# A four-layer conditional residual block: second sums computed already turned, identity inside the adapter weights, and another order of the first part

## The chip, the cores and the metric

The kernel runs on one core of one Trainium2 chip. The metric is the device time of one execution in microseconds; the number quoted for a kernel is the median of its runs. A profile is one further execution, recorded by the hardware profiler, and it comes with its own time.

## The reference, cut to what matters

The input x has 32 sequences of 32 tokens with 512 features, all in float32. Four layers each add their result to x:

```python
x = x + einsum('bct,bcd->bdt', x, w_mix[cond])                          # 1: mixes the 32 tokens of a sequence
x = x + einsum('bsi,oi->bso', x, W) + 0.5 * ((x @ lora_A[lab]) @ lora_B.T)   # 2: base product and LoRA
x = x + einsum('bsi,boi->bso', x, weight[adapter_id])                   # 3: one 512x512 adapter per sequence
x = x + attention(x)     # 4: q, k, v projections, norms, rotary turn, paged cache of 512 keys, output product
```

Layers 1 to 3 and a part of layer 4's value projection are the first part of the kernel, which the change rewrites. The adapter weights are 32 times 1 MB, one for each sequence, chosen by an index.

## The kernel before, in words

The 1024 tokens are cut into eight tiles of 128 tokens (four sequences a tile). `xs` holds all tiles with tokens on the partitions. Three stages follow one another: the first part (layers 1 to 3 and seven tiles of one value chunk), a second part of query, key and value projections in blocks of two tiles (line L393), and the attention with the output product.

For tile t the first part does the following.

- `mixers(t)` (L674, L681) builds on VectorE a 128x128 block matrix of the four gathered mixing weights with the identity added; `mix(t)` (L688) multiplies with it, so that the residual is in the product, and leaves the tile turned (features on the partitions) in `x1t`.
- `low_1(t)` (L707) multiplies by the LoRA matrices of all five labelers; VectorE picks one (L711, L718) into a wide tile whose other columns are zero.
- `base(t)` (L726) multiplies 128 tokens by `wb`, which has the identity on its diagonal, with 512 output columns moving; L729 turns the low values, L731 scales them, L732 adds the LoRA product. VectorE copies the sum back to `xs` (L734).
- `flip_2(t)` (L697, x2t) turns the sum with four TensorE transposes, and ScalarE copies it.
- `adapt(t)` (L751) multiplies each sequence's 32 tokens by its own adapter weight, four column groups side by side; VectorE adds the product to `xs` (L758).
- `transposed(t, x3t)` (L697) turns the result for the projections; after every second tile `token_sums` (L375 to L378) forms four sums on GpSimd.
- `project` (L312) computes a value tile of chunk NCH - 2, copied by ScalarE (L322) and stored by GpSimd's queue (L327).

TensorE and VectorE run the first part in the order in which the code is written (`manual_schedule`); ScalarE, GpSimd and the SP queue are ordered by the planner of the framework. In the second part and in the attention, all engines run in written order. The written loop of the first part takes, at step n, mix(n), base(n-1), flip_2(n-2), low_1(n), the turn of tile n-4, adapt(n-3) and value tiles from n = 6 on. `angles()` computes the rotary sines and cosines: VectorE first (L764 to L781), then ScalarE (L778 to L783), then eight products on GpSimd (L789 to L792).

All large loads go through the SP queue. An adapter weight `wa` has eight buffers, so `load_adapt` for tile t+2 waits until adapt(t) has read its buffers. `load_qkv` loads the value chunk's weight (1024 KB), and `load_pair(0)` the first pair of the second part (2 MB in four loads).

Of the kernel before, what the change touches and what calls it, by code (L numbers as in the profile page):

```python
# [12 lines left out]
F32 = mybir.dt.float32  # L13
# [7 lines left out]
P = 128  # L21
# [38 lines left out]
def cond_resid_kernel(  # L60
# [227 lines left out]
    taken = []  # L288

    def accumulator(name: str, long: bool = False):  # L290
        taken.append(name)
        pool = ps_m if long or len(taken) % 3 else ps_n
        return pool.tile([P, HID], F32, tag="mm", name=name)


    x3_all = xp.tile([P, KC, NT * P], F32, name="x3t")

    def x3t(t: int):
# [331 lines left out]
    with ExitStack() as p1:  # L630
# [8 lines left out]
        lb = w1p.tile([P, HID], F32, name="lb")  # L639
        nc.gpsimd.memset(lb, 0.0)  # L640

        ones = w1p.tile([P, HID], F32, name="ones")
        nc.vector.memset(ones, 1.0)
# [7 lines left out]
        mgs, x1ts, lows, x2ts, was = {}, {}, {}, {}, {}  # L651


        wide = [w1p.tile([P, P], F32, name=f"low_{i}") for i in range(3)]
        for low in wide:
            nc.gpsimd.memset(low, 0.0)

        def gather_mix(t: int):
            mg = sp.tile([P, S], F32, tag="mg", name=f"mg_{t}", bufs=4)
# [10 lines left out]
        def mixers(t: int):  # L670


            md = sp.tile([P, BT, S], F32, tag="md", name=f"md_{t}", bufs=3)
            nc.vector.tensor_tensor(  # L674
                md,
                mgs.pop(t).unsqueeze(1).to_broadcast([P, BT, S]),
                quarter.unsqueeze(2).to_broadcast([P, BT, S]),
                ALU.mult,
            )
            mds[t] = md.rearrange("p j s -> p (j s)")  # L680
            nc.vector.tensor_tensor(mds[t], mds[t], ident, ALU.add)  # L681

        def mix(t: int):

            md = mds.pop(t)
            px = ps_tr.tile([P, KC, P], F32, tag="tr", name=f"x1t_ps_{t}")
            for k in range(KC):
                nc.tensor.matmul(  # L688
                    px[:, k, :], xs[:, t, k * P : (k + 1) * P], md, start=True, stop=True
                )  # L690
            x1ts[t] = sp.tile([P, KC, P], F32, tag="x1t", name=f"x1t_{t}", bufs=3)
            nc.scalar.copy(x1ts[t], px)
# [9 lines left out]
        which = w1p.tile([P, NT, NL], F32, name="which")  # L702

        def low_1(t: int):
            plo = ps_m.tile([P, HID], F32, tag="mm", name=f"low_ps_{t}")[:, : NL * R]
            for k in range(KC):
                nc.tensor.matmul(  # L707
                    plo, x1ts[t][:, k, :], la[:, k, :], start=(k == 0), stop=(k == KC - 1)
                )
# [12 lines left out]
        def base(t: int):  # L722
            xt = x1ts.pop(t)
            pb = accumulator(f"base_{t}")
            for k in range(KC):
                nc.tensor.matmul(pb, xt[:, k, :], wb[:, k, :], start=(k == 0), stop=False)  # L726
                if k == KC - 2:
                    plt = ps_tr.tile([P, P], F32, tag="tr", name=f"lowt_ps_{t}")
                    nc.tensor.transpose(plt, lows.pop(t), ident)  # L729
                    lowt = sp.tile([P, P], F32, tag="lowt", name=f"lowt_{t}")  # L730
                    nc.scalar.mul(lowt, plt, LORA_SCALING)  # L731
            nc.tensor.matmul(pb, lowt, lb, start=False, stop=True)  # L732

            nc.vector.tensor_copy(xs[:, t, :], pb)  # L734

        def flip_2(t: int):
            x2ts[t] = sp.tile([P, KC, P], F32, tag="x2t", name=f"x2t_{t}")
            transposed(t, x2ts[t], "x2t")

        def load_adapt(b: int):  # L740
            was[b] = wap.tile([P, KC, HID], F32, tag="wa", name=f"wa_{b}")
            dma_picked(was[b], w_adapt, pk[0:1, b : b + 1], "a p k o -> p (a k) o")

        def adapt(t: int):
            xt = x2ts.pop(t)
            pa2 = accumulator(f"adapt_{t}")

            for k in range(KC):
                for j in range(BT):
                    r = slice(j * S, (j + 1) * S)  # L750
                    nc.tensor.matmul(  # L751
                        pa2[r, :],
                        xt[:, k, r],
                        was[t * BT + j][:, k, :],
                        start=(k == 0),
                        stop=(k == KC - 1),
                    )
            nc.vector.tensor_tensor(xs[:, t, :], xs[:, t, :], pa2, ALU.add)  # L758

        def angles():  # L760

# [12 lines left out]
            for part in (PI_A, PI_B, PI_C):  # L774
# [7 lines left out]
            cs = w1p.tile([P, NT, H2], F32, name="cs")  # L782
            nc.scalar.activation(  # L783
                cs.rearrange("p t f -> p (t f)"), turns, AF.Sin, bias=half_pi, scale=-1.0
            )
# [15 lines left out]
        loads = ExitStack()  # L801
        loads.enter_context(tc.issue_after(gate.ins))
        load_x(2)
        nc.sync.dma_start(out=lb[:R, :], in_=lora_b)
        load_x(3)
        for b in range(BT):
            load_adapt(b)
# [15 lines left out]
        with tc.manual_schedule(engines={mybir.EngineType.PE, mybir.EngineType.DVE}):  # L823

            idle = ps_tr.tile([P, HID], F32, tag="tr", name="idle_ps")
            for n in (HID, HID, P, P, P, P, P, P):
                nc.tensor.matmul(idle[:, :n], ones[:, :P], ones[:, :n], start=True, stop=True)

            def ahead_of(t: int):
                if t + 3 < NT:  # L830
                    gather_mix(t + 3)
                if t < NT:
                    mixers(t)

            def adapt_and_load(t: int):
                adapt(t)
                if t + 2 < NT:
                    for j in range(BT):
                        load_adapt((t + 2) * BT + j)
# [12 lines left out]
            low_1(1)  # L852
            base(0)
            mix(2)
            low_1(2)
            ahead_of(3)
            flip_2(0)
            base(1)
            for n in range(3, NT + 4):
                if n < NT:  # L860
                    mix(n)
                if n - 1 < NT:
                    base(n - 1)
                if n - 2 < NT:
                    flip_2(n - 2)
                if n < NT:
                    low_1(n)
                    ahead_of(n + 1)
                if NT <= n:
                    project(NCH - 2, n - 6 + (n == NT + 3))  # L870
                if n == NT + 2:
                    project(NCH - 2, NT - 3)
                if 0 <= n - 4 < NT:
                    transposed(n - 4, x3t(n - 4), "x3t")
                    if n % 2:
                        token_sums((n - 4) // 2)
                if n - 3 < NT:
                    adapt_and_load(n - 3)
                if n == 3:
                    constants()  # L880
                    angles()
                if 6 <= n < NT:
                    project(NCH - 2, n - 6)
                if n == 4:
                    with tc.issue_after(picked[-1]):
                        load_qkv(NCH - 2)
                if n == 6:
                    with tc.issue_after(picked[-1]):
                        load_pair(0)

    nc.gpsimd.dma_start(out=x_d.rearrange("t p d -> p t d"), in_=xs)
    first_part.close()
# [507 lines left out]
```

## Time and profile before

| what | value |
|---|---|
| median of 3 runs | 1136.5 us (1135.73 to 1137.75) |
| the profiled execution's own time | 1136.3 us |
| its span | 1134.5 us |
| granted TensorE clock, mean | 1.0 |
| first part ends (first L393 product begins) | 121.66 us |
| adapters begin, tiles 0 to 7 | 31.14, 42.17, 53.61, 64.64, 79.10, 95.01, 103.04, 114.11 us |
| DMA bytes over the span | 259.24 MB, mean 229 GB/s |

The page gives each engine's busy time over the span; TensorE's matmuls are pipelined and their ends are modelled. Every float32 matmul appears as two passes, so "x32" beside an adapter means 16 matmuls. In a timeline the columns are start and length in us, engine, line, operation, what is written from what, the shape, the count, and in brackets the idle time ahead with what ended it. In a table of windows each engine's busy time and instruction count stand in the order PE, PEld (weight load), DVE (VectorE), ACT (ScalarE), POOL (GpSimd), then the granted clock, the mean busy share of the 16 DMA engines and GB/s.

### The profile page before, as it was taken

What the parts mean: (1) busy time and instruction counts of PE and PEld (TensorE: products, weight loads), DVE (VectorE), ACT (ScalarE), POOL (GpSimd) and SP (SyncE); (2) the same over time, 40 slices, a digit from 0 to 9 for tenths busy, and PEclk for the clock granted to TensorE, in tenths of its full rate; (3) what the DMA queues carried; (4) which work ended last, traced back from release to release, by engine and by line L of the source; (5) the groups of instructions that cost most, each with busy time, mean ns of one, the idle gap of its engine ahead of it and who ended that gap; (6) DMA issues with size and microseconds to landing.
All of it is one profiled execution on the core that took longest, in us unless ns stands there. A gap on an engine that the chain in (4) does not pass through costs nothing.

```text
span 1134.5 us, 19093 instructions
## 1 busy us (share of the span) xinstructions
PE 1119.1 (99%) x5480; PEld 738.0 (65%) x5480; DVE 812.3 (72%) x1674; ACT 739.3 (65%) x1885; POOL 561.0 (49%) x730
## 2 busy tenths in 40 slices
PE   8999999999999899999999999999999999999998
PEld 5554444444444688777777777777777777777766
DVE  2510688887877578878778878887877787877861
ACT  1211377676666677678877777777777877777850
POOL 3411689899798455543444344334433443344410
PEclk9999999999999999999999999999999999999999
DMA  8998447688886687778767756775777676766600
GB/s 319 391 419 352 177 130 211 162 246 221 210 234 176 203 267 264 254 255 301 241 210 243 260 190 212 264 244 183 234 239 240 199 234 223 253 201 212 231 28 10
DMA packets 173355, 259.24 MB, mean 229 GB/s; under 512 B 31522, under 2 KB 130466, under 8 KB 168770
## 3 DMA queue, kind: packets, MB, share of 16 engines
q1 hardware_dynamic: 152226, 184.22, 51.4%
q0 software_dynamic: 20016, 71.97, 17.8%
q10 hardware_dynamic: 1008, 1.84, 0.4%
q8 instruction: 44, 0.72, 0.3%
q14 instruction: 61, 0.50, 0.1%
HBM read 228.46 MB, written 37.88 MB: 235 GB/s over the span
## 4 chain that ended last, share of the span: by engine, by line
PE 61%; DVE 2%; ACT 0%; issue 0%; DVEq 0%
PE o_ps L1103 19%; PE f_ps L1180 18%; PE s_ps L1023 11%; PE s_ps L1024 9%; PE o_ps L1123 2%; PE pn_ps L1090 1%; PE f_ps L1200 1%; PE f_ps_last L1200 1%; DVE placed L1079 1%; PE qkv L312 1%; DVE pr L1032 0%; DVE turned L1061 0%; ACT placed L1075 0%; DVE os L1139 0%; DVE ot L1160 0%
## 5 line engine op out<-in xcount | busy, mean ns | idle before, releaser
L1075 ACT COPY placed<-turned 32x512 f32<-32x512 f32 x524 | 322.6, 616 | 30.2 <-DVE turned L1061 24.2
L1103 PEld LDWEIGHTS o_ps<-vt,placed 128*128 128x128 f32 x2048 | 264.2, 191 | 110.9 <-issue 74.6
L1032 DVE CUSTOM_DVE_ANT_0 pr<-s_ps,mask,rq 128x544 f32<-128x544 f32 x256 | 200.4, 783 | 129.6 <-PE s_ps L1024 106.4
L1048 ACT ACTIVATE pr<-pr,low 128x544 f32<-128x544 f32 x256 | 191.6, 748 | 142.6 <-DVE low L1032 116.1
L1077 POOL COPY placed<-turned 32x512 f32<-32x512 f32 x279 | 169.6, 608 | 222.2 <-DVE turned L1061 173.5
L1103 PE MATMUL o_ps<-vt,placed 128*128 128x128 f32 x2048 | 272.0, 276 | 3.9 <-DVE os L1139 3.3
L1180 PE MATMUL f_ps<-wo,ot 128*128 128x512 f32 x480 | 240.6, 593 | 0.0
L1061 DVE STREAM_TRANSPOSE turned<-pr 128x512 f32<-128x512 f32 x256 | 178.6, 698 | 0.1
L1023 PE MATMUL s_ps<-kt,qt 128*128 128x288 f32 x512 | 174.0, 421 | 4.2 <-DVE low L1032 2.4
L1024 PE MATMUL s_ps<-kt,qt 128*128 128x256 f32 x512 | 152.3, 379 | 0.0
L252 POOL DMA_INDIRECT vt<-in_v_cache_dram,v_idx x128 | 124.3, 971 | 36.6 <-issue 25.7
L1024 PEld LDWEIGHTS s_ps<-kt,qt 128*128 128x128 f32 x512 | 97.3, 190 | 26.8
L438 POOL TENSOR_TENSOR ra<-ra,rs 128x512 f32<-128x512 f32 x80 | 103.8, 1303 | 10.7 <-DVE rs L433 8.1
L1079 DVE COPY placed<-turned 32x512 f32<-32x512 f32 x221 | 101.9, 461 | 5.6
L1180 PEld LDWEIGHTS f_ps<-wo,ot 128*128 128x128 f32 x480 | 86.9, 190 | 25.1 <-issue 13.9
L1086 POOL COPY pq<-pr 128x128 f32<-128x128 f32 x64 | 18.5, 288 | 151.6 <-ACT pr L1048 111.2
L1023 PEld LDWEIGHTS s_ps<-kt,qt 128*128 128x128 f32 x512 | 78.2, 191 | 17.3 <-DVE low L1032 6.1
L451 ACT ACTIVATE sq<-x 128x128 f32<-128x128 f32 x256 | 76.2, 301 | 19.8 <-DVE x L409 13.6
L548 ACT COPY r<-m 128x512 f32<-128x512 f32 x80 | 46.3, 579 | 52.4 <-PE m L393 50.4
L393 PE MATMUL m<-t_pair,x_sums 128*128 128x512 f32 x160 | 75.4, 594 | 0.7 <-ACT r L548 0.7
L393 PE MATMUL m<-w_pair,x3t 128*128 128x512 f32 x160 | 75.2, 592 | 0.0
L393 PE MATMUL m<-w_pair,x_sums 128*128 128x512 f32 x160 | 72.1, 593 | 0.0
(129 smaller groups left out, 1231.8 us busy)
## 6 DMA issues: line engine op xcount, KB each, us to landing
kt<-in_k_cache_dram SPq DMA_DIRECT2D x512, 128.0 KB
wa<-in_w_adapt_dram SPq DMA_DIRECT2D x32, 1024.0 KB
q_d<-st SPq DMA_DIRECT2D x128, 128.0 KB
qt<-q_d SPq DMA_DIRECT2D x64, 256.0 KB
w_pair<-in_w_qkv_dram SPq DMA_DIRECT2D x20, 512.0 KB
o_d<-in_w_o_dram SPq DMA_DIRECT2D x16, 512.0 KB
wo<-o_d SPq DMA_DIRECT2D x16, 512.0 KB
k_d<-st SPq DMA_DIRECT2D x32, 128.0 KB
```

What stands on the lines that cost most here:

```text
L252: nc.gpsimd.indirect_dma_start(out=vts[b][:, c, :], out_offset=None, in_=v_cache, in_offset=bass.IndirectOffsetOnAxis(ap=v_idx[:, at : at ...
L393: nc.tensor.matmul(ps, of[:, k], by[:, k], start=(not more and k == 0), stop=(k == KH - 1), skip_group_check=more,)
L1023: nc.tensor.matmul(ps[:, first:L], q, kt4[:, :N_LOW, g, :], start=True, stop=True)
L1024: nc.tensor.matmul(ps[:, L : first + LT], q, kt4[:, N_LOW:, g, :], start=True, stop=True)
L1032: nc.vector.tensor_tensor_reduce(pr, ps[:, first : first + LT], mask, rqs[b][:, g // QUAD, u : u + 1], 3.0e38, ALU.add, ALU.min, low,)
L1048: nc.scalar.activation(pr, pr, AF.Exp, bias=low, scale=-1.0, accum_out=dens[quad][:, u : u + 1])
L1061: nc.vector.transpose(part, pr)
L1075: nc.scalar.copy(dst, src)
L1077: nc.gpsimd.tensor_copy(dst, src)
L1079: nc.vector.tensor_copy(dst, src)
L1103: nc.tensor.matmul(po, pt[:, c, :], vt[:, c, g * D : (g + 1) * D], start=(c == 0 and q == 0), stop=(c == L // P - 1 and q == 1),)
L1180: nc.tensor.matmul(pfs[t][:, :HID], ots[t, h // HALF][:, h % HALF, :], wo(h), start=(h == 0), stop=(h == (HQ if t < NT - 1 else HALF) - 1),)
```

## The change

- `base` works on two tiles and computes the sum already turned: pieces of `wb` are the stationary side and 256 tokens move. The low values are repeated four times across the columns, so that after one transpose each of four groups of 32 partitions holds them, and the LoRA product is four matmuls of 32 rows each. ScalarE copies the four sums into `x2t`. `flip_2` and the copy to `xs` are gone.
- `with_identity` adds the identity to the four adapter weights of a tile on VectorE, two operations a weight; `adapt` then yields x plus the product, and VectorE copies it to `xs`.
- The written order of the first part is a list: two base products come ahead of the first adapter, mixes and low products run in twos, `angles` moves behind adapt(4), and value tiles 3 to 6 stand behind the last adapter.
- `load_qkv` follows the loads of tile 2, and `load_pair(0)` the loads of tile 7. `lora_b` is loaded in four pieces. Buffers of `mg` and `md` grow by one; accumulators of base are in one pool, those of low products, adapters and value tiles in another.

```diff
-    def project(c: int, t: int, slots=()):
-        ps = accumulator(f"qkv_{c}_{t}", True)
+    def project(c: int, t: int, slots=(), pool=ps_m):
+        ps = pool.tile([P, HID], F32, tag="mm", name=f"qkv_{c}_{t}")
...
-            lows[t] = wide[t % 3]
+            lows[t] = sp.tile([P, KC, R], F32, tag="low", name=f"low_{t}")
             nc.vector.tensor_reduce(
-                lows[t][:, :R], picked.rearrange("p l r -> p r l"), AX.X, ALU.add
+                lows[t][:, 0, :], picked.rearrange("p l r -> p r l"), AX.X, ALU.add
+            )
+            nc.vector.tensor_copy(
+                lows[t][:, 1:, :], lows[t][:, 0, :].unsqueeze(1).to_broadcast([P, KC - 1, R])
             )
...
+        def base(g: int):
+            xt = x1ts.pop(g)
+            pbs = [
+                ps_m.tile([P, HID], F32, tag="mm", name=f"base_{g}_{j}")[:, : 2 * P]
+                for j in range(KC)
+            ]
+            lowt = sp.tile([P, 2 * P], F32, tag="lowt", name=f"lowt_{g}")
+            for j in range(KC):
+                for k in range(KC):
+                    nc.tensor.matmul(pbs[j], wb[:, k, j * P : (j + 1) * P], xt[:, k, :],
+                                     start=(k == 0), stop=False)
+                if j == KC - 2:
+                    plt = ps_tr.tile([P, 2 * P], F32, tag="tr", name=f"lowt_ps_{g}")
+                    for u in range(2):
+                        low = lows.pop(2 * g + u).rearrange("p j r -> p (j r)")
+                        nc.tensor.transpose(plt[:, u * P : (u + 1) * P], low, ident)
+                    nc.scalar.mul(lowt, plt, LORA_SCALING)
+            x2ts[g] = sp.tile([P, KC, 2 * P], F32, tag="x2t", name=f"x2t_{g}")
+            for j in range(KC):
+                r = slice(j * R, (j + 1) * R)
+                nc.tensor.matmul(pbs[j], lb[r, :], lowt[r, :], start=False, stop=True)
+            for j in range(KC):
+                nc.scalar.copy(x2ts[g][:, j, :], pbs[j])
...
+        def with_identity(t: int):
+            for b in range(t * BT, (t + 1) * BT):
+                w = was[b].rearrange("p k o -> p (k o)")
+                step = HID + P
+                most = w[:, : (KC - 1) * step].rearrange("p (k o) -> p k o", o=step)[:, :, :P]
+                last = w[:, (KC - 1) * step :]
+                one = ident.unsqueeze(1).to_broadcast([P, KC - 1, P])
+                nc.vector.tensor_tensor(most, most, one, ALU.add)
+                nc.vector.tensor_tensor(last, last, ident, ALU.add)
...
-            nc.vector.tensor_tensor(xs[:, t, :], xs[:, t, :], pa2, ALU.add)
+            nc.vector.tensor_copy(xs[:, t, :], pa2)
...
+            ahead_of(3)
+            ahead_of(4, 5)
             base(0)
+            mixed(2, 3)
+            ahead_of(6)
+            with_identity(0)
             base(1)
+            adapt(0)
+            loads(2)
+            with tc.issue_after(picked[-1]):
+                load_qkv(NCH - 2)
+            with_identity(1)
+            turned(0)
+            adapt(1)
+            loads(3)
+            mixed(4, 5)
+            turned(1)
+            with_identity(2)
+            constants()
+            adapt(2)
+            loads(4)
+            ahead_of(7)
+            with_identity(3)
+            base(2)
+            turned(2)
+            adapt(3)
+            loads(5)
+            values_of(0)
+            mixed(6, 7)
+            with_identity(4)
+            turned(3)
+            adapt(4)
+            loads(6)
+            angles()
+            with_identity(5)
+            base(3)
+            turned(4)
+            adapt(5)
+            loads(7)
+            with tc.issue_after(picked[-1]):
+                load_pair(0)
+            with_identity(6)
+            values_of(1)
+            turned(5)
+            adapt(6)
+            with_identity(7)
+            values_of(2)
+            turned(6)
+            adapt(7)
+            values_of(3)
+            values_of(4)
+            turned(7)
+            values_of(5)
+            values_of(6)
```

`mixed(*tiles)` runs mix for the tiles and then low_1 for them, `turned(t)` is the turn of tile t with its token sums, `values_of(t)` a value tile, and `loads(t)` the four adapter loads of a tile.

More of the change, by code (lines that the diff above doesn't have):

```diff
@@ L287, in cond_resid_kernel @@
     ps_tr = flips.enter_context(tc.tile_pool(name="a_tr", bufs=2, space=PSUM, side="right"))
[L288 to L293, printed above, removed]
     x3_all = xp.tile([P, KC, NT * P], F32, name="x3t")
@@ L638, in cond_resid_kernel @@
         la = w1p.tile([P, KC, NL * R], F32, name="la")
-        lb = w1p.tile([P, HID], F32, name="lb")
-        nc.gpsimd.memset(lb, 0.0)
+        lb = w1p.tile([P, P], F32, name="lb")
         ones = w1p.tile([P, HID], F32, name="ones")
@@ L651, in cond_resid_kernel @@
         mgs, x1ts, lows, x2ts, was = {}, {}, {}, {}, {}
-        wide = [w1p.tile([P, P], F32, name=f"low_{i}") for i in range(3)]
-        for low in wide:
-            nc.gpsimd.memset(low, 0.0)
         def gather_mix(t: int):
-            mg = sp.tile([P, S], F32, tag="mg", name=f"mg_{t}", bufs=4)
+            mg = sp.tile([P, S], F32, tag="mg", name=f"mg_{t}", bufs=5)
             nc.gpsimd.indirect_dma_start(
@@ L670, in mixers @@
         def mixers(t: int):
-            md = sp.tile([P, BT, S], F32, tag="md", name=f"md_{t}", bufs=3)
+            md = sp.tile([P, BT, S], F32, tag="md", name=f"md_{t}", bufs=4)
             nc.vector.tensor_tensor(
@@ L690, in mix @@
                 )
-            x1ts[t] = sp.tile([P, KC, P], F32, tag="x1t", name=f"x1t_{t}", bufs=3)
-            nc.scalar.copy(x1ts[t], px)
+            g, u = divmod(t, 2)
+            if u == 0:
+                x1ts[g] = sp.tile([P, KC, 2 * P], F32, tag="x1t", name=f"x1t_{g}")
+            nc.scalar.copy(x1ts[g][:, :, u * P : (u + 1) * P], px)
         def transposed(t: int, dst: bass.AP, name: str):
@@ L704, in low_1 @@
         def low_1(t: int):
-            plo = ps_m.tile([P, HID], F32, tag="mm", name=f"low_ps_{t}")[:, : NL * R]
+            g, u = divmod(t, 2)
+            plo = ps_n.tile([P, HID], F32, tag="mm", name=f"low_ps_{t}")[:, : NL * R]
             for k in range(KC):
                 nc.tensor.matmul(
-                    plo, x1ts[t][:, k, :], la[:, k, :], start=(k == 0), stop=(k == KC - 1)
+                    plo,
+                    x1ts[g][:, k, u * P : (u + 1) * P],
+                    la[:, k, :],
+                    start=(k == 0),
+                    stop=(k == KC - 1),
                 )
@@ L716, in low_1 @@
             )
-            lows[t] = wide[t % 3]
+            lows[t] = sp.tile([P, KC, R], F32, tag="low", name=f"low_{t}")
             nc.vector.tensor_reduce(
-                lows[t][:, :R], picked.rearrange("p l r -> p r l"), AX.X, ALU.add
+                lows[t][:, 0, :], picked.rearrange("p l r -> p r l"), AX.X, ALU.add
             )
[L722 to L730, printed above, removed]
-                    nc.scalar.mul(lowt, plt, LORA_SCALING)
-            nc.tensor.matmul(pb, lowt, lb, start=False, stop=True)
-            nc.vector.tensor_copy(xs[:, t, :], pb)
@@ L736, in flip_2 @@
-        def flip_2(t: int):
-            x2ts[t] = sp.tile([P, KC, P], F32, tag="x2t", name=f"x2t_{t}")
-            transposed(t, x2ts[t], "x2t")
+            nc.vector.tensor_copy(
[10 more added lines that the diff above has]
+                for k in range(KC):
+                    nc.tensor.matmul(
+                        pbs[j],
+                        wb[:, k, j * P : (j + 1) * P],
+                        xt[:, k, :],
+                        start=(k == 0),
+                        stop=False,
+                    )
+                if j == KC - 2:
[3 more added lines that the diff above has]
+                        nc.tensor.transpose(plt[:, u * P : (u + 1) * P], low, ident)
+                    nc.scalar.mul(lowt, plt, LORA_SCALING)
+            x2ts[g] = sp.tile([P, KC, 2 * P], F32, tag="x2t", name=f"x2t_{g}")
[4 more added lines that the diff above has]
+                nc.scalar.copy(x2ts[g][:, j, :], pbs[j])
@@ L742, in load_adapt @@
             dma_picked(was[b], w_adapt, pk[0:1, b : b + 1], "a p k o -> p (a k) o")
+        def with_identity(t: int):
[7 more added lines that the diff above has]
+                nc.vector.tensor_tensor(last, last, ident, ALU.add)
         def adapt(t: int):
-            xt = x2ts.pop(t)
-            pa2 = accumulator(f"adapt_{t}")
+            g, u = divmod(t, 2)
+            xt = x2ts[g][:, :, u * P : (u + 1) * P]
+            pa2 = ps_n.tile([P, HID], F32, tag="mm", name=f"adapt_{t}")
             for k in range(KC):
@@ L781, in angles @@
             nc.vector.scalar_tensor_tensor(turns, af, -1.0, af, ALU.mult, ALU.max)
[L782 to L785, printed above, removed]
+            cs = ang
+            nc.scalar.activation(af, turns, AF.Sin, bias=half_pi, scale=-1.0)
             for i in range(2):
@@ L803, in cond_resid_kernel @@
         load_x(2)
-        nc.sync.dma_start(out=lb[:R, :], in_=lora_b)
+        for j in range(KC):
+            nc.sync.dma_start(
+                out=lb[j * R : (j + 1) * R, :], in_=lora_b[:, j * P : (j + 1) * P]
+            )
         load_x(3)
@@ L827, in cond_resid_kernel, with mixed, ahead_of, loads @@
                 nc.tensor.matmul(idle[:, :n], ones[:, :P], ones[:, :n], start=True, stop=True)
[L829 to L832, printed above, removed]
-                    mixers(t)
[L835 to L839, printed above, removed]
+            def mixed(*tiles):
+                for t in tiles:
+                    mix(t)
+                for t in tiles:
+                    low_1(t)
+            def ahead_of(*tiles):
+                for t in tiles:
+                    if t + 3 < NT:
+                        gather_mix(t + 3)
+                    mixers(t)
+            def loads(t: int):
+                for j in range(BT):
+                    load_adapt(t * BT + j)
+            def turned(t: int):
+                transposed(t, x3t(t), "x3t")
+                if t % 2:
+                    token_sums(t // 2)
+            def values_of(t: int):
+                project(NCH - 2, t, (), ps_n)
             ahead_of(0)
@@ L852, in cond_resid_kernel @@
             low_1(1)
+            ahead_of(3)
+            ahead_of(4, 5)
             base(0)
[L854 to L857, printed above, removed]
+            mixed(2, 3)
+            ahead_of(6)
+            with_identity(0)
             base(1)
[L859 to L889, printed above, removed]
```

## The prediction

> **What bounds the kernel now.** I read the page first (engine shares, then the slices), because it says which engine is never free. TensorE is busy 99% of the span:
>
> ```profile
> span 1134.5 us, 19093 instructions
> PE 1119.1 (99%) x5480; PEld 738.0 (65%) x5480; DVE 812.3 (72%) x1674; ACT 739.3 (65%) x1885; POOL 561.0 (49%) x730
> ```
>
> The change lies in the first part alone, so next came the timeline of TensorE from 0 to 190 us. The part ends at 121.66 us, where the first L393 product stands; from there to 300 us TensorE idles under 1 us, so whatever the first part gains or loses moves all the rest with it. These are the adapters that set the loads free, and that end:
>
> ```profile
> 31.14 3.64 PE L751 MATMUL adapt<-wa,x2t 128*32 128x512 f32 x32
> ...
> 95.01 3.64 PE L751 MATMUL adapt<-wa,x2t 128*32 128x512 f32 x32
> ...
> 114.11 3.64 PE L751 MATMUL adapt<-wa,x2t 128*32 128x512 f32 x32
> 117.69 3.70 PE L312 MATMUL qkv<-wq,x3t 128*128 128x512 f32 x8
> 121.22 0.60 PE L697 MATMUL x3t_ps<-ident,xs 128*128 128x128 f32 x4
> 121.66 1.88 PE L393 MATMUL m<-w_pair,x3t 128*128 128x512 f32 x4
> ```
>
> TensorE has no hole there, but it is not alone. The stage windows show the DMA engines full from 12 to 96 us (their share and GB/s are the last two columns):
>
> ```profile
> 12.00:36.00 24.00, 23.33 (x114) 12.85 (x115) 7.57 (x23) 3.26 (x8) 1.66 (x2) 1.00 1.02 407
> 36.00:60.00 24.00, 23.63 (x139) 12.14 (x138) 12.99 (x30) 7.49 (x13) 12.92 (x12) 1.00 0.99 389
> 60.00:96.00 36.00, 36.00 (x178) 17.32 (x180) 5.47 (x11) 6.59 (x13) 4.41 (x7) 1.00 1.01 419
> ```
>
> So two resources run side by side: TensorE, and the stream of 32 adapter weights of 1024 KB. A tile's four weights (4.19 MB) take 10 us, and their eight buffers are two tiles deep: the load of tile t+2 waits for adapt(t). Last, the timeline of VectorE, since the change gives it work that TensorE will wait for:
>
> ```profile
> 34.93 0.69 DVE L758 TENSOR_TENSOR xs<-xs,adapt 128x512 f32<-128x512 f32 x1 [2.35 <-PE adapt L751]
> ...
> 43.62 1.18 DVE L674 TENSOR_TENSOR md<-mg,quarter 128x128 f32<-128x128 f32 x1
> 44.83 1.25 DVE L681 TENSOR_TENSOR md<-md,ident 128x128 f32<-128x128 f32 x1
> ```
>
> VectorE is mostly free (5.47 of 36 us from 60 to 96). But the two md operations, 0.29 us at their median, took 1.2 us when GpSimd ran L792 and L791 (from 43.36 us, 1.3 us each): each ended only after a GpSimd operation had.
>
> **The change, part by part.** All sums are against the profiled execution (1136.3 us, span 1134.5; the median of the runs is 1136.5, so both stand within 0.2 us).
>
> TensorE's savings. flip_2 goes: eight times 0.44 us (40.12 to 40.55) = 3.5 us. Base passes now move 256 columns, twice as many at half of 0.43 us: no change; 6.87 us a pair of tiles, and 0.22 us for two transposes. The LoRA product had 0.86 us a tile, 1.72 a pair; now eight passes with 32 rows each, four row groups side by side. The nearest row is L1123 (32 rows, 128 columns): 16 passes from 402.13 to 402.78, 0.041 us each where a full 128-column pass takes 0.11. By that ratio, eight passes of 256 columns cost 0.6 us; without overlap 1.72. I take 0.6: a base pair is 7.7 us. If TensorE never waited, its chain would run: base(0) at 11.96 as now, two mixes and two low products 4.0, base(1) 7.7, so adapt(0) at 31.35 (now 31.14), adapt(5) ending at 82, the part at 111.6: 10 us earlier. Evictions of base move from VectorE (0.69 us) to ScalarE in 256-column copies of about 0.38; ScalarE is busy 6.59 of 36 us, and its next reader is a base product away. At nothing; bare, 4 x 0.38 us a pair.
>
> VectorE's new work. with_identity is two adds a weight. 128 columns: 0.286 (L850); 1024 columns: 1.22 (L367 at 118.43); 384 by interpolation 0.55. L850's four adds took 0.90 together, so each hides 0.08: 0.68 us a weight, 2.8 a tile (3.4 without that hiding). What matters is its place. Both engines' order is written by hand, VectorE's runs in it (L734 for tile 3 waited until 42.31 behind the angles), and with_identity(t) stands behind the eviction of adapt(t-1). The eviction starts 0.21 us after adapt's end and the next operation 0.60 later (34.72, 34.93, 35.53). So adapt(t) can't begin before 0.81 + 2.8 us past the adapt before it, plus whatever else is queued between on VectorE:
> - adapt(1): 34.9 + 3.6 = 38.5, ends 42.1. TensorE has only turned(0) meanwhile: 3.1 us of stall.
> - adapt(2): mixed(4, 5) ends at 46.1, low_1(5) with the new copy needs VectorE until 47.2, then 2.8: 50.0. token_sums(0) (four GpSimd adds, 2.9 us) starts about 47.4, right across. One VectorE add per GpSimd add, as the md rows did: +1.5; held out wholly: +2.9; no clash: 0. With 1.5: 51.5, ends 55.1.
> - adapt(3): base(2) and turned(2) end at 63.3; its weights land at 60.3 (21.65 MB by the windows, wq now ahead of them), their last identity by 61.5. No stall; ends 66.9.
> - adapt(4): value tile 3.5, mixed(6, 7) 4.0, low_1(7) until 75.5, identity 2.8, token_sums(1) +1.5 (0 to 2.9): 79.8, ends 83.4 (now 82.7). All of TensorE's lead is gone.
> - adapt(5): behind the eviction stand the angles, 6.1 us (35.83 to 42.31 less a 0.5 mask): VectorE reaches with_identity(5) at 90.3. The sines are ready at 91.9, and GpSimd then runs eight multiplications of 1.27 (43.36 to 53.35). Half of the eight adds are through by then; four go one per multiplication, 5.1 us for 1.4. So 96.8 instead of 93.1 (held out wholly: 103); TensorE is ready at 91.6. I take 96.8, the row being the same operations on both engines; adapt(5) ends at 100.4.
>
> The loads. Tile 7's are set free by adapt(5). Now they go out at 98.6 and the traffic ends about 111.2 (378 GB/s to 108, 333 in the next 4 us, 88 after that): 12.6 us from release to landing. The first pair's load moves behind them, so at 80 us nothing fills the queue any more: tile 5 lands at 80.4, tile 6 is released at 83.4. With release at 100.4, tile 7 lands at 113.0, identity to 113.8, adapt(7) ends at 117.4. Two value tiles and two turned ones fit before it.
>
> The end. Behind adapt(7) now stand four value tiles (3.45 each) and one turned tile: 14.3 us, where one of each stands now. The part ends at adapt(5)'s end + 12.6 + 0.8 + 3.6 + 14.3 = +31.3, that is 131.7 us against 121.66. Today the same distance is 121.66 - 98.6 = 23.1. So the break-even is plain: adapt(5) must end by 90.4.
>
> Edits at nothing: the pair's weights and weight sums, late in the queue, have the 14 us of values as cover (bare: up to 5 us for 2 MB); four small lb loads in place of one on SP (0.35 us of issue each, landed long before base(0) needs them near 19 us); three memsets less on GpSimd. x_d's store and pair 1 start with adapt(7)'s end, as now, and gain slack. GpSimd's stores of values wait behind the multiplications, two buffers deep, with 7 us of TensorE between them.
>
> Sum: +10.0 us by these terms; 1136.3 + 10 = 1146.
>
> One rule speaks for less: the Trainium skill, "SBUF — State Buffer", section "Who interferes with whom", says that the shared pair of ports is held for one instruction and the second comer waits it out; by it each clash costs at most one GpSimd operation, near my sum. This trace also has a 128x512 VectorE sum at 124.21 that took 4.32 us across several GpSimd operations, which is more than the rule gives and is why I keep "held out wholly" as an end.
>
> Another speaks against the change: "TensorE: Matmul & The Clock Gate", section "Why this matters for your kernels", warns of idle gaps over about 3 us, after which the clock falls to half. The trace has such a pace only at the start, 512-column passes of 1.10 us (L827) against 0.59; no later gap is long enough to show it. If the rule held for the three or four stalls of 3 to 5 us, an estimate from the page's 3.4 us of rewarming would be 1.7 us for each, some 5 us more.
>
> **The rivals.**
> - Identity stays hidden and the stream decides. The other side: 39.0 MB must land before adapt(7) can run; 2.44 are there at 12 us, and 36.6 at 415 GB/s end at 100.1. Then 0.9 + 3.6 + 14.3: 118.9, a gain of 2.8 us (1133.5). It needs adapt(5) out by about 88, so stalls of at most 6 us on TensorE's chain; VectorE's written order speaks against it, its low load for it.
> - Stalls, but no clash with GpSimd (its work placed elsewhere): 10 less 1.5, 1.5 and 3.7, +3.3 us (1139.6). For it: only GpSimd, ScalarE and SP are free in order here.
> - VectorE held out wholly, or TensorE slow after stalls: +2.8 for the two sums, +6 at the angles, up to 5 for a slow pace: 1150 to 1158. For it, the 4.32 us sum.
>
> **How the numbers follow.** About 0.2% (2.3 us) is what a measurement can tell from no change. Forecast 0.55, hidden identity 0.10, no clash 0.20, held out or slow 0.15. The no-clash case falls within 0.2% a quarter of the time (0.05), the hidden one a fifth (0.02): same 0.07, faster 0.08, slower 0.85. The range runs from the no-clash case less the 0.4 us a tile that faster identity adds would spare over five tiles, 1137.5, to the middle of the last case, 1154.
>
> **What would show it.** Stalls of TensorE ahead of adapt(1), (2), (4) and (5), put down to VectorE's identity adds; such adds of 0.3 to 0.6 us, over 0.7 beside GpSimd; a dip of DMA traffic near 82 and 97 us; adapt(5) ending near 100; 14 us of values behind adapt(7). It is wrong if adapt(5) ends before 90.4, or if with_identity runs ahead of the evictions.

## The result, and the profile after

The changed kernel takes 1149.57 us (median of 5 runs, 1147.67 to 1149.97) against 1136.5 (also 5 runs, 1135.73 to 1137.75): ratio 1.011 with an interval of 1.0097 to 1.0122, 13.1 us slower. The forecast was 1146.0, in a range of 1137.5 to 1154. The profiled execution took 1149.97 us (span 1148.2), 13.7 more than that of before.

The first lines of the page: TensorE's busy time grows by 5 us only, and VectorE's by 25. The span grows because TensorE waits; some of the waiting is even counted as busy, as in adapt(1), begun at 38.05 while VectorE was still at its weights and listed with 5.51 us where adapt(0) took 3.64.

```profile
span 1148.2 us, 19268 instructions
PE 1124.4 (98%) x5528; PEld 747.9 (65%) x5528; DVE 837.5 (73%) x1738; ACT 738.8 (64%) x1889; POOL 563.3 (49%) x726
```

TensorE's timeline, with the lines that answer to those of before (adapt(0), (4), (5), (6), (7), then the last values). Where an adapter is split in groups, its end is that of its last group:

```profile
32.94 3.64 PE L770 MATMUL adapt<-wa,x2t 128*32 128x512 f32 x32
...
80.38 6.60 PE L770 MATMUL adapt<-wa,x2t 128*32 128x512 f32 x30 [0.66 <-DVE wa L759]
...
98.46 3.62 PE L770 MATMUL adapt<-wa,x2t 128*32 128x512 f32 x26 [1.78 <-DVE wa L759]
...
110.02 3.62 PE L770 MATMUL adapt<-wa,x2t 128*32 128x512 f32 x26 [1.73 <-DVE wa L759]
...
117.64 3.64 PE L770 MATMUL adapt<-wa,x2t 128*32 128x512 f32 x32
121.21 7.13 PE L304 MATMUL qkv<-wq,x3t 128*128 128x512 f32 x16
128.18 0.60 PE L686 MATMUL x3t_ps<-ident,xs 128*128 128x128 f32 x4
128.61 7.03 PE L304 MATMUL qkv<-wq,x3t 128*128 128x512 f32 x16
135.48 1.88 PE L385 MATMUL m<-w_pair,x3t 128*128 128x512 f32 x4
```

adapt(5) ends at 102.1, 3.4 us later than before (95.01 + 3.64 = 98.65), and the part at 135.48 instead of 121.66: 13.8 us, the whole loss. Behind adapt(7) stand 14.3 us of values and turning. TensorE's waits up to 140 us name the identity adds (L759) as the releaser; "issue" holds two waits of 1.24 us ahead of adapt(2) and adapt(4), which are gone in the run without the adds below:

```profile
PE adapt L770 <- DVE wa L759: 5.1, 6, 1.8
PE adapt L770 <- issue: 2.5, 2, 1.2
```

The windows (columns as before) show the stream run dry where tiles are set free late: it is still full from 12 to 60 us, moves 39 GB/s at 84 to 88, and has a mean busy share of 0.40 and 0.41 from 96 to 104:

```profile
36.00:60.00 24.00, 20.90 (x125) 10.61 (x118) 14.18 (x36) 2.34 (x4) 3.86 (x4) 1.00 0.99 403
...
80.00:84.00 4.00, 3.62 (x11) 0.88 (x15) 2.93 (x6) 0.00 (x0) 2.03 (x2) 0.57 0.45 192
84.00:88.00 4.00, 4.00 (x28) 2.00 (x21) 0.95 (x3) 0.00 (x0) 0.00 (x0) 1.00 0.25 39
96.00:100.00 4.00, 2.22 (x22) 0.55 (x20) 3.69 (x3) 1.89 (x6) 4.00 (x4) 1.00 0.40 168
100.00:104.00 4.00, 4.00 (x19) 1.38 (x12) 1.88 (x3) 0.00 (x0) 4.00 (x4) 1.00 0.41 123
```

VectorE's timeline gives the reason at with_identity(5), which comes behind the angles, and with_identity(6):

```profile
93.69 0.55 DVE L759 TENSOR_TENSOR wa<-wa,ident 128x384 f32<-128x384 f32 x1
...
95.50 1.37 DVE L760 TENSOR_TENSOR wa<-wa,ident 128x128 f32<-128x128 f32 x1
96.79 1.61 DVE L759 TENSOR_TENSOR wa<-wa,ident 128x384 f32<-128x384 f32 x1
98.33 1.36 DVE L760 TENSOR_TENSOR wa<-wa,ident 128x128 f32<-128x128 f32 x1
102.12 0.69 DVE L777 COPY xs<-adapt 128x512 f32<-128x512 f32 x1 [2.43 <-PE adapt L770]
...
103.62 1.35 DVE L760 TENSOR_TENSOR wa<-wa,ident 128x128 f32<-128x128 f32 x1
104.89 1.62 DVE L759 TENSOR_TENSOR wa<-wa,ident 128x384 f32<-128x384 f32 x1
...
107.11 2.38 DVE L760 TENSOR_TENSOR wa<-wa,ident 128x128 f32<-128x128 f32 x1
```

GpSimd's timeline over the same stretch, its first and last products of the angles and the token sums of tiles 4 and 5 behind them:

```profile
95.08 2.91 POOL L809 TENSOR_TENSOR sw<-sn,nw 128x512 f32<-128x512 f32 x2 [12.97 <-ACT sn L797]
...
104.78 1.32 POOL L808 TENSOR_TENSOR sw<-nsn,nw 128x512 f32<-128x512 f32 x1
...
107.25 0.73 POOL L367 TENSOR_TENSOR x_sums<-x3t 128x256 f32<-128x256 f32 x1
107.93 0.73 POOL L369 TENSOR_TENSOR x_sums<-x3t 128x256 f32<-128x256 f32 x1
108.61 0.72 POOL L368 TENSOR_TENSOR x_sums<-x_sums,x3t 128x256 f32<-128x256 f32 x1
```

Alone, the adds take 0.55 and 0.28 us. From 95.08 to 106.1, while GpSimd makes the eight products of the angles (L806 to L809), most of them take 1.35 to 1.62. The add of 2.38 us, at 107.11, comes after the products: it lies beside three token sums and ends 0.16 us after the third. with_identity(5) lasts 6.0 us and with_identity(6) 8.0 (102.73 to 110.70) instead of 2.75. Of the 5.2 us that with_identity(6) takes too long, its first three adds, beside the products, hold 2.6, and the two adds beside token sums the other 2.6.

### The profile page after: what moved, and what is told of

It reads as the page before. It is cut to its first block, busy times and chain, and to the rows that moved or that the text cites. A ratio compares the mean times of both kernels' runs of the same rounds, so it can differ in the third digit from the quotient of the medians.

```text
span 1148.2 us, 19268 instructions
## 1 busy us (share of the span) xinstructions
PE 1124.4 (98%) x5528; PEld 747.9 (65%) x5528; DVE 837.5 (73%) x1738; ACT 738.8 (64%) x1889; POOL 563.3 (49%) x726
## 4 chain that ended last, share of the span: by engine, by line
PE 60%; DVE 2%; ACT 0%; issue 0%; DVEq 0%
PE o_ps L1150 19%; PE f_ps L1227 18%; PE s_ps L1070 11%; PE s_ps L1071 9%; PE o_ps L1170 2%; PE pn_ps L1137 1%; PE f_ps L1247 1%; PE f_ps_last L1247 1%; DVE placed L1126 1%; PE qkv L304 1%; DVE pr L1079 0%; DVE turned L1108 0%; ACT placed L1122 0%; DVE os L1186 0%; DVE ot L1207 0%
## 5 line engine op out<-in xcount | busy, mean ns | idle before, releaser
L1122 ACT COPY placed<-turned 32x512 f32<-32x512 f32 x524 | 322.5, 616 | 30.3 <-DVE turned L1108 24.3
```

Of the source, the lines that this page charges most:

```text
L1122: nc.scalar.copy(dst, src)
```

## Experiments

The theory: the loss is the place of VectorE's identity adds (behind evictions, low products and angles) and their clash with GpSimd; both delay adapt(5), whose end sets tile 7's loads free. The rivals: a slow TensorE clock after the stalls, the longer end behind adapt(7) by itself, and the pair's loads in the stream. The runs were made in three groups on three chips; each is compared with the kernel before in its own group (1136.3, 1139.07, 1130.99 us). Figures such as "adapt(5) ends" come from each run's profiled execution.

**No identity adds.** The eight calls go, so the adapters leave out their identity part; all else stays.

```diff
-            with_identity(0)
... (and 1 to 7)
```

> The changed kernel without with_identity: the residual of the second layer is left out of the third layer's sum, all else stays. Theory (VectorE's identity adds, queued behind evictions, hold up the adapters and with them the loads): no stall of TensorE ahead of adapters but for DMA; adapt(5) ends near 90 us instead of 102.0, the first part ends near 121 us instead of 135.5, the time falls by 12 to 15 us to about 1136, level with the kernel before. Rival (the turned base product, the load order or the values at the end cost the time): the first part still ends past 131 us, at most 4 us come back.

Measured: 1135.72 us, ratio 0.9998 (0.9988 to 1.0007). TensorE's timeline in this run, then its waits:

```profile
86.17 3.64 PE L770 MATMUL adapt<-wa,x2t 128*32 128x512 f32 x32
...
104.26 3.62 PE L770 MATMUL adapt<-wa,x2t 128*32 128x512 f32 x26 [1.75 <-DMA wa<-in_w_adapt_dram]
...
122.09 1.88 PE L385 MATMUL m<-w_pair,x3t 128*128 128x512 f32 x4
```

```profile
PE adapt L770 <- DMA wa<-in_w_adapt_dram: 3.6, 3, 1.7
```

All 13 us are the adds'. The rest of the change is worth nothing here: adapt(5) ends at 89.8, 8.8 us before it did in the kernel before, but tile 7 lands some 14.4 us later and 14.3 us of values follow, so the part ends where it did.

**Angles before the first base product**, so that neither they nor the products stand near adapt(5); their two inputs are loaded ahead of the adapter weights.

```diff
             ahead_of(4, 5)
+            constants()
+            angles()
             base(0)
```

> angles (with constants) stand before base(0), where VectorE idles, and their two small inputs are loaded ahead of the first adapter weights. Theory: with_identity(5) no longer waits 6.1 us behind them and GpSimd's eight products no longer meet with_identity(5) and (6); adapt(5) starts when TensorE is ready (95.5 us, ends 99.1 instead of 102.0), with_identity(6) takes 3 to 4 us instead of 8, the part ends about 5 us sooner (1144 to 1146). Rival (the stream of weights decides, since tile 7 is released by adapt(5) and must still land 12.6 us later): no more than the 2.9 us of adapt(5) come back, 1146.5 or more.

Measured: 1149.06 us, 1.0113 (1.0096 to 1.013); the expected 1144 to 1146 was missed, and the rival's bound of 1146.5 or more held. The products now ran from 24.3 to 34.6 us, straight across with_identity(0) (30.62 to 36.6), so the clash had been moved, not removed; adapt(0) took 4.64 us instead of 3.64. A second wait came with the move: ScalarE's sines now stood ahead of its copy of a mixed tile (L681, at 24.65 us where the changed kernel had it at 22.16), TensorE waited 3.1 us for it, and adapt(0) began 2.5 us later. adapt(5) no longer waited, but with the start so much later it still ended at 101.8, and what the short with_identity(6) would have given back went to tile 7, whose last weight came 14.9 us after adapt(5)'s end. So this run does not tell the products' price.

**Token sums after the last adapter** in the code.

```diff
-                if t % 2:
-                    token_sums(t // 2)
...
             adapt(7)
+            for p in range(NP - 1):
+                token_sums(p)
```

> All token sums on GpSimd move behind adapt(7); nothing else changes. Theory (the shared clash of VectorE and GpSimd lengthens the identity adds): with_identity(2) and (4) take 2.8 us each instead of 4.9, so adapt(4) ends near 82.7 instead of 86.9 and the part ends about 4 us sooner (1145 to 1146). Rival (the clash only fills time that VectorE waits anyway): the adds shorten but the part ends within 1 us of 135.5.

Measured: 1148.91 us, 1.0117 (1.01 to 1.0134). This is no test: the first sum began at 48.14 us where the changed kernel had it at 48.97, and with_identity(2) still took 4.9 us. GpSimd's order here is the planner's, not that of the calls.

**Identity adds sooner:** with_identity(4) ahead of the mixes, with_identity(5) ahead of the angles.

```diff
             values_of(0)
+            with_identity(4)
             mixed(6, 7)
-            with_identity(4)
...
+            with_identity(5)
             angles()
-            with_identity(5)
```

> Only VectorE's written order changes: with_identity(4) stands ahead of mixed(6, 7), with_identity(5) ahead of the angles. Same work on every engine. Theory (place, not amount): adapt(4) starts when TensorE is ready, near 77.4 us, ends near 81 instead of 86.9; adapt(5) ends near 93 instead of 102; GpSimd's eight products then meet with_identity(6), which stays at 6 to 8 us; the part ends near 127, the time is 1140 to 1143. Rival (amount of VectorE work, or the stream): less than 3 us come back, 1146.5 or more.

Measured: 1143.64 us, 1.0068 (1.0051 to 1.0084), just above the expected 1140 to 1143; the two moves are worth about 5 us by the ratios. That is not place alone, since they also took with_identity(4) out of the token sums and with_identity(5) out of the products. adapt(4) and adapt(5) ended at 80.5 and 92.6 as expected, without a wait. But with_identity(6) now met the products. VectorE's timeline, then GpSimd's, over the same stretch:

```profile
93.89 1.35 DVE L760 TENSOR_TENSOR wa<-wa,ident 128x128 f32<-128x128 f32 x1
95.17 1.62 DVE L759 TENSOR_TENSOR wa<-wa,ident 128x384 f32<-128x384 f32 x1
96.71 1.35 DVE L760 TENSOR_TENSOR wa<-wa,ident 128x128 f32<-128x128 f32 x1
```

```profile
95.06 1.31 POOL L808 TENSOR_TENSOR sw<-nsn,nw 128x512 f32<-128x512 f32 x1
96.33 1.58 POOL L806 TENSOR_TENSOR cw<-ang,nw 128x512 f32<-128x512 f32 x1
97.88 1.30 POOL L807 TENSOR_TENSOR cw<-ang,nw 128x512 f32<-128x512 f32 x1
```

The two engines take turns, one for one: the products end at 96.37 and 97.91, and the adds begun ahead of those ends are through 0.42 us (384 columns) and 0.15 us (128 columns) after them, at 96.79 and 98.06. Each add waits for a product and then runs. with_identity(6) took 10 us. The Trainium skill, "SBUF — State Buffer", section "Who interferes with whom", says that whichever of two such operations issues first keeps the shared ports for its whole length while the other is blocked; these rows agree for a single operation, and show that a series pays it every time.

**Spare matmuls in the stalls** ahead of adapt(2) and adapt(4), three of 128x512 each, against the slow clock.

```diff
             with_identity(2)
+            keep_busy(0)
...
             turned(3)
+            keep_busy(1)
```

> The changed kernel with three spare 128x512 matmuls (2.6 us) in each of the two long stalls, ahead of adapt(2) and adapt(4). Theory: the stalls themselves cost the time and the slow clock after them is small; the clock no longer falls near 82 us (0.57 from 80 to 84 in the changed kernel), adapt(4) ends 0.6 us sooner, the time stays within 2 us of 1149.5. Rival (the clock that falls in the stalls is a main cost): 4 us or more come back, 1145.5 or less.

Measured: 1149.91 us, 1.0093 (1.0078 to 1.0107). The product behind adapt(4) began at 86.06 instead of 86.91, the granted clock of 80 to 84 us was 1.00, and the time hardly moved (the interval meets the change's own), so a slow clock is not a main cost. The slow pace is real but small: in the changed kernel the granted clock of 80 to 84 us was 0.57, and from the end of the last 384-column add to the end of the adapter it took 4.19 us at adapt(4) (82.72 to 86.91) and 3.60 at adapt(2), so 0.6 us.

**No clash at (2) and (6)** (the earlier identity adds as above): token sums 0 wait on with_identity(2), the products on with_identity(6).

```diff
+            sums = turned(1)
+            behind(with_identity(2), *sums)
...
+            behind(with_identity(6), *made)
```

> e5's order of VectorE, and GpSimd's work made to wait: the first token sums behind with_identity(2), the eight products of the angles behind with_identity(6). Theory (besides place, the clash of VectorE and GpSimd costs): with_identity(2) takes 2.8 us instead of 4.9, with_identity(6) 2.8 instead of 10; adapt(6) starts when TensorE is ready (near 94.6 us, ends 98.2), tile 7 lands about 14.5 us after adapt(5)'s end as in the runs without identity and with early angles; the part ends near 123.5, the time is 1137 to 1139. Rival (clash only fills waiting time, as moving the angles seemed to show): no more than 2 us below e5, 1141.5 or more.

Measured: 1145.32 us, 1.0063 (1.0041 to 1.0084); the expected 1137 to 1139 was missed, and the time lies in the rival's range. with_identity(2) took 2.8 us instead of 4.9, adapt(5) ended at 90.3. But the clash was not gone: the products met with_identity(7), which took 11 us (98.69 to 109.8), and TensorE then went on at a lower clock. TensorE's timeline and the window (same columns):

```profile
108.55 6.25 PE L773 MATMUL adapt<-wa,x2t 128*32 128x512 f32 x26 [1.76 <-DVE wa L761]
```

```profile
108.00:112.00 4.00, 3.45 (x20) 0.83 (x24) 1.77 (x2) 0.00 (x0) 2.15 (x3) 0.50 0.23 84
```

Here the clock costs 2.6 us: 26 passes take 6.25 us at 0.50 and 3.62 at full pace.

**The pair's loads last:** the run above, with the first pair's weights waiting on with_identity(7).

> e8, and the first pair's loads wait for with_identity(7) instead of being issued right behind tile 7's. Theory (the pair's 2 MB share the DMA engines with tile 7's last weights, and make its landing 14.5 us after release instead of the 12.6 of the kernel before): tile 7 lands 2 us sooner, adapt(7) and the part's end follow by 1.5 to 2 us: 1135 to 1137. Rival (loads are served in order, the pair costs tile 7 nothing): within 0.5 us of e8.

Measured: 1148.34 us, ratio 1.0062 (1.0041 to 1.0083), single times from 1142.61 to 1149.68; the expected 1135 to 1137 was missed. Inconclusive: adapt(7) was held by the products again, so the landing of tile 7 decided nothing.

**A new order of the whole part:** with_identity(1) and with_identity(4) a step earlier, two adapters before the first turn, the value weight's load behind tile 3's, the angles behind the last mixes, values_of(3) before adapt(7), token sums 0 and the pair's loads waiting as above. Two pieces of the edit:

```diff
+            with_identity(1)
             adapt(0)
...
+            values_of(3)
             adapt(7)
```

> All of it: with_identity(1) ahead of adapt(0)'s eviction and adapt(1) ahead of turned(0); the value weight behind tile 3 instead of tile 2; with_identity(4) ahead of mixed(6, 7); angles behind mixed(6, 7); the first token sums behind with_identity(2); the pair's loads behind with_identity(7); value tile 3 ahead of adapt(7). Theory: TensorE waits only for landings; adapt(5) ends near 88 us, adapt(7) near 107 with 10.8 us behind it, the part ends near 118 against 121.7 in the kernel before: 1131 to 1134, faster than both. Rival (the stream of weights, 39 MB at 415 GB/s, or two VectorE adds a weight keep it level): 1135 to 1138.

Measured: 1144.95 us, 1.006 (1.0042 to 1.0078); the expected 1131 to 1134 was missed. With the angles earlier, the products met with_identity(5) (83.10 to 94.0), and adapt(5) ended at 96.4:

```profile
92.77 3.62 PE L775 MATMUL adapt<-wa,x2t 128*32 128x512 f32 x26 [1.76 <-DVE wa L763]
```

**The products last, alone:** the changed kernel, its eight products waiting on with_identity(7).

```diff
-            angles()
+            made = angles()
...
-            with_identity(7)
+            behind(with_identity(7), *made)
```

> The changed kernel, with only one thing made different: GpSimd's eight products of the angles wait for with_identity(7). Theory (the products lengthen with_identity(5) and (6) by taking turns with them): with_identity(5) and (6) take 2.8 us each instead of 6 and 8; adapt(5) ends near 99.6 instead of 102.0, adapt(6) near 107 instead of 113.6; tile 7, released by adapt(5), then decides, 14.5 us later; the part ends near 133, 2 to 3 us sooner than the changed kernel, that is 8 to 11.5 us slower than the kernel before on the same chip. Rival (clash only fills waiting time): within 1 us of the changed kernel, 12 us or more slower than before.

Measured: 1140.28 us, 1.0081 (1.0066 to 1.0096), 9.3 us slower than before, as expected (8 to 11.5). with_identity(5) and (6) took 2.75 us each, adapt(5) ended at 99.2 and tile 7's last weight stood at 111.76, 12.5 us later. With with_identity(6) done by 102.6, token sums of tiles 4 and 5 (from 104.37) no longer met it either. So the products' clash, with what it brought on, is 13.1 - 9.3 = 3.8 us; the intervals of the two ratios leave about 2 us either way. The rest is place, values, the token sums at with_identity(2) and (4), and a slow pace, not separated here.

**The new order with the products last:** the new order of the whole part, its eight products waiting on with_identity(7), the pair's loads right behind tile 7's in one run and waiting on with_identity(7) in the other.

> All of e10's order, with the eight products behind with_identity(7), but the first pair's loads issued right behind tile 7's as in the changed kernel. If the pair's 2 MB share the DMA engines with tile 7: tile 7 lands 14.5 us after adapt(5)'s end, adapt(7) ends 1.5 to 2 us later than in the next run. If loads are served in order: the same within 0.5 us.

> e10's order, with the eight products behind with_identity(7) and the pair's loads behind it too. Theory: with no clash left, adapt(5) ends near 89.4, tile 7 lands near 102, adapt(7) ends near 108, the part ends near 119 against 121.7 in the kernel before: 1 to 4 us faster than the kernel before on the same chip. Rival (the weight stream, or waits on VectorE not seen yet, keep it level): within 1 us of the kernel before, or slower.

Measured: 1128.96 us, 0.9979 (0.9969 to 0.9988), and 1128.30 us, 0.9975 (0.9965 to 0.9985). Both beat the kernel before, the second by 2.7 us. TensorE's timeline of the second (adapt(5), adapt(7), the part's end), then VectorE's last weight:

```profile
86.47 3.64 PE L775 MATMUL adapt<-wa,x2t 128*32 128x512 f32 x32
...
105.18 3.88 PE L775 MATMUL adapt<-wa,x2t 128*32 128x512 f32 x32
...
119.83 1.88 PE L389 MATMUL m<-w_pair,x3t 128*128 128x512 f32 x4
```

```profile
104.83 0.56 DVE L763 TENSOR_TENSOR wa<-wa,ident 128x384 f32<-128x384 f32 x1 [1.81 <-DMA wa<-in_w_adapt_dram]
```

adapt(5) ends at 90.1, now without a stall; adapt(7) begins as soon as value tile 3 ends, with its last weight landed at 104.83, so it is held by no add, and 10.8 us follow it instead of 14.3. Where the pair's loads stand makes no difference that these runs tell. Against the run with only the products moved, where the part ends at 130.20, it ends 10.4 us sooner: 9.1 by adapt(5), 3.4 by the value tile ahead of adapt(7), less 2.2 because tile 7 came 14.7 us after its release instead of 12.5.

## Why the prediction was right, and where its size was off

**The mechanism held.** Identity adds on VectorE delay the adapters, adapt(5)'s end releases tile 7, and everything after is carried: taking the adds away returned all the time, and undoing place, clash and end together made the kernel faster than before. The dips of DMA traffic stood near 82 and 97 us as named. TensorE's own savings came as costed: the LoRA passes took 0.64 us a pair (0.6 predicted), a tile's adds 2.76 us alone (2.8), the end behind adapt(7) 14.27 us (14.3).

**The sum was 3.8 us short** (part end 135.48 against 131.7). By the steps:

- adapt(4) ended at 87.0 instead of 83.4. Of these 3.6 us, 1.6 were there at adapt(0), which began at 32.94 and not at 31.35. The chain was reckoned as if TensorE never waited, but base(0) began at 13.10 and not at 11.96: the second low product waited 1.6 us, until ScalarE's copy of its tile (L681), begun at 11.27 where it stood at 9.33 before, was through. Nor could base(0) have begun much sooner, since the mixing weights of the third gather reached VectorE at 11.54 us (9.36 before) and the identity for `wb`, which follows them there, was added by 13.0. Why both came later stays open. The rest of the 1.6 is a base pair of 7.87 us instead of 7.7, twice, and 0.1 at the mixes. The token sums cost 2.1 us at with_identity(2) and at (4) (4.9 us for 2.75) where 1.5 was taken, 1.2 in all, and the slow clock 0.6; about 0.2 us is left over.
- From there adapt(5) took 15.1 us instead of 17.0, because the clash with the products cost 2.2 us at this place and not 3.7 (12.9 in the run with the products last).
- From adapt(5)'s end to the part's end it was 33.4 us instead of 31.3. This step failed in kind: the clash was priced at with_identity(5) only, while the products, from 95.08 to 106.1, also covered the first adds of with_identity(6) and so pushed its last ones into the token sums of tiles 4 and 5; it took 8 us. So TensorE's chain and not tile 7's landing decided when adapt(7) ran. With the products out of the way the leg was 31.0, as reckoned.

The products' clash was thus split otherwise than forecast. That its whole came near the 3.7 us taken (3.8 by the medians, 2.2 + 2.4 by these steps) is partly luck: one place was priced too high and the other at nothing. The other terms that were too small are the start and the sums.

**The rivals.** The hidden identity was not this kernel's case. The last run comes near it, with one value tile moved as well: adapt(5) out at 90.1, the part's end at 119.8 where the rival had 118.9. The case without a clash, +3.3 us, would be +6.3 if only the products' 3.7 are left out; measured were +9.3, over by some 3 us, nearly all of it there at adapt(4), which in that run ended at 86.2 instead of 83.4. "Held out wholly" did not occur at the identity adds beside the products, where turns were taken, but VectorE operations were held through several of GpSimd's elsewhere: the add of 2.38 us through three token sums, and in the last two runs a sum of the pair's weights through the whole rest of the products. VectorE's line with the pair's loads waiting, then with them right behind tile 7's:

```profile
111.98 6.12 DVE L361 TENSOR_TENSOR t_pair<-w_pair 128x1024 f32<-128x1024 f32 x1 [2.19 <-DMA w_pair<-in_w_qkv_dram]
```

```profile
109.07 8.59 DVE L359 TENSOR_TENSOR t_pair<-w_pair 128x1024 f32<-128x1024 f32 x1
```

Such a sum took 1.22 us in the kernel before; here the last products ended at 116.62 and 116.17 us and the sums 1.5 us behind them. TensorE did not wait for either. The estimate of 5 us for a slow clock, made from the Trainium skill, "TensorE: Matmul & The Clock Gate", section "Why this matters for your kernels", was too high for the changed kernel: of two stalls alike one was followed by a slow pace, for 0.6 us.

## What to carry to other kernels

An operation that moves to an engine with a fixed order is priced by what stands ahead of it there and by which loads its reader sets free, not by its busy time: eight times 2.75 us of adds on an engine that was busy 26 of 84 us in this part (12 to 96 us, before) cost 13. Before moving a two-operand VectorE operation, list what GpSimd runs at that time; here, pushing a long row of GpSimd products to another place only moved the clash until it stood behind the last add that anyone waits for. On an engine that a planner orders, moving the call in the code moved nothing (48.97 to 48.14 us); a dependency did.

## What the runs showed of the hardware that was not expected

- A series of VectorE adds with both operands in SBUF and a series of two-operand GpSimd products can take turns one for one. Eight adds went from 2.75 us to 10 or 11, and some products from 1.27 to 1.58. It is no rule: the rows of 2.38, 6.12 and 8.59 us above were held through three or more GpSimd operations in a row. What decides between the two stays open.
- The granted clock after a stall is not regular: after the same pattern of waits it was 1.00 in adapt(2) (48 to 56 us) and 0.57 in adapt(4) (80 to 84 us). With only the products moved it was the other way round, 0.84 and 0.73 in adapt(2) and 1.00 in adapt(4); in the run with the products behind with_identity(6) it fell to 0.50.
- Four 1 MB weights land 12.5 to 14.9 us after their release, in runs that differ in what else is queued; moving the pair's loads did not change it. Part may be the stream itself: it still ran at 430 GB/s (88 to 90 us) when tile 7 was released in the last run (14.7 us), and had run down to 57 GB/s (98 to 100 us) with only the products moved (12.5). But with the angles early it had run down too (82 GB/s, 100 to 102 us) and the loads took 14.9, so what decides stays open.
